# A cross-attention block on one core: the set-up copies, the constants' transfers and the last norms are rearranged

## The chip, the cores and the metric

The kernel runs on one core of one Trainium2 chip. The metric is the time of one execution on the device in microseconds (us). Engines are named as in the profile: PE is TensorE (matmuls; PEld its weight loads), DVE is VectorE, ACT is ScalarE, POOL is GpSimd, SP is SyncE, which here only issues transfers. ACT issues some transfers too; rows called SPq and ACTq are those issues. Each engine works through its own list of instructions strictly in the order in which the program gives them.

## The reference

One layer: 128 sequences of 128 tokens, model width 256, 16 heads of 16, feed-forward width 1024, everything float32.

```python
q = (x @ Wq + bq) ; k = (ctx @ Wk + bk) ; v = (ctx @ Wv + bv)      # 16 heads of 16
scores = einsum('bhqd,bhkd->bhqk', q, k) / sqrt(16)
scores = where(j < i, scores, -1e30)       # strictly below the diagonal
attn = softmax(scores); attn[:, :, 0, :] = 0
x1  = layer_norm(x + (attn @ v) @ Wo + bo, ln1_g, ln1_b)
out = layer_norm(x1 + relu(x1 @ W1 + b1) @ W2 + b2, ln2_g, ln2_b)
# layer_norm(t) = (t - mean) * (var + 1e-5) ** -0.5 * g + b
```

## The kernel before, in words

**Tiling.** Two sequences make a pair, and 64 pairs (p = 0 to 63) are worked through one after the other, software-pipelined by hand: while pair p has its scores and softmax, pair p-1 has its context, output projection and first norm, pair p-2 the first feed-forward matmul (`hidden`, result `hT`, through PSUM tile `ph`) and pair p-3 the second (`second`, PSUM tile `py`) with the last norm. The order on PE, DVE, ACT and POOL is the order of the calls in the program text; nothing is rescheduled.

**Softmax of a pair.** `scores(p, hi)` gives the upper (hi = 1) or lower half of the query rows in PSUM tile `pss`; DVE adds the mask tile `neg` while moving them to SBUF tile `sm` (L351), takes the negated maximum `nmx` (L362), POOL adds it (L363), ACT takes the exponential (L370), DVE sums (L382) and inverts (L383), and POOL multiplies (L384). The `sm` tiles have one buffer each. The weights are then turned: for most pairs by DVE and transfers (`turn`), for the first two and for part of the last on PE (`turn_on_pe`: four transposes into PSUM tile `ptp` at L426, then an ACT copy to `pT` at L428). `weigh` (PSUM `pc`), `context` (ACT, `cxT`) and `attention_out` (PSUM `po`) follow.

**Set-up.** Inputs come by transfers in the order of the text: on SP's queue the first tokens `x`, `wq`, `c_first` (the first pair's context), three `column` vectors (`bq_c`, `bk_c`, `b1_c`), weights `wk`, `wv`, `w1`, the blocks `xb`, `cb` of pair 1 (four transfers each), `wo`, rows, and the blocks of pairs 2 and 3; on ACT's queue three `chunks` (`bv_c`, `g1_c`, `be1_c`) and a copy of half of the mask, `neg` to `neg` (L169). Every transfer bears one of eight semaphores in rotation over both queues, and each issue waits until the transfer eight places earlier has landed. So the mask's copy waits for `be1_c`, and `wk` for `bv_c`; whatever is behind such a wait on its queue waits too. For pair 0, PE transposes `x` into `ptx` (L234), ACT copies it to `xT` (L671), PE projects queries into `pq` (L268), and then the same is done with `c_first` (`ptc`, `cT`) for the keys, `pk`. ACT moves `pq` to `qT` with bias `bqs_c` (L279) and `pk` to `kT` with `bkh` and `half` (L290). From pair 1 on, DVE makes `xT` and `cT` from the blocks (`tokens`, L253). `fold_norm1` (PSUM `ps_b`, L561) multiplies `w1` with `be1_c`; `fold_values` (`ps_bv`, L577; `bov_r`, L580) needs `bvw`, made from `bv_c`.

**Small PSUM tiles** (`bank`) share four buffers in rotation: `ptx`, `pq`, `pv`, `pc`, `po`, `ph`, `py`, `ptp` all come from them, and a matmul into a buffer waits until its previous content has been read.

**End.** In the last pair's turn of the loop (`end`) the lists are: `store` of an earlier pair's rows on ACT's queue, stats, `scale_and_shift` on POOL, then one half of `hidden(61)`, the transposes of pair 63's upper scores, the other half of `hidden(61)`, then `norm2` on ACT. After the loop pairs 61, 62 and 63 are finished one after the other; pair 62's last norm goes through `scale_and_shift` (POOL), `norm2` (ACT, L539), `finish` (POOL, L545 and L546); pair 63's goes sequence by sequence through the code at L886 to L904 on DVE and POOL, with a `pow` on POOL at L898.

Of the kernel before, what the change touches and what calls it, by code (L numbers as in the profile page):

```python
# [8 lines left out]
F32 = mybir.dt.float32  # L9
AF = mybir.ActivationFunctionType  # L10
ALU = mybir.AluOpType
AX = mybir.AxisListType

P = 128
NEG_INF = -1e30
# [4 lines left out]
def tile_cross_attention_block(  # L20
# [22 lines left out]
    nc = tc.nc  # L43
# [5 lines left out]
    KC = D // P  # L49
# [5 lines left out]
    HP = P // 2  # L55
    QSCALE = 1.0 / DK ** 0.5
# [6 lines left out]
    const = ctx.enter_context(tc.tile_pool(name="const", bufs=1))  # L63
# [11 lines left out]
    states = {}  # L75


    blocks_of, tokens_of = {}, {}
# [18 lines left out]
    def load_tokens(g, us=slice(0, 4)):  # L97
        if g not in tokens_of:
            tokens_of[g] = loads.tile([P, 4, D], F32, tag="x", name=f"x_{g}")
        nc.sync.dma_start(  # L100
            tokens_of[g][:, us], x[4 * g + us.start : 4 * g + us.stop].rearrange("b p d -> p b d")
        )


    def weight(w, name):
        n = w.shape[0] // P
        t = const.tile([P, n, w.shape[1]], F32, tag=name, name=name)
        nc.sync.dma_start(t, w.rearrange("(k p) n -> p k n", p=P))
        return t

    def column(v, name):
        t = const.tile([P, v.shape[1]], F32, tag=name, name=name)
        nc.sync.dma_start(t, v)
        return t

    def chunks(v, name):
# [4 lines left out]
    def row(v, name):  # L121
# [2 lines left out]
        return t  # L124

    load_tokens(0, slice(0, 2))
    c_first = const.tile([P, 2, D], F32, tag="c_first", name="c_first")
    wq = weight(Wq, "wq")
    nc.sync.dma_start(c_first, c[0:2].rearrange("b p d -> p b d"))
    bq_c = column(bq, "bq_c")  # L130
    bk_c = column(bk, "bk_c")
    wk = weight(Wk, "wk")
    wv = weight(Wv, "wv")
    ident = const.tile([P, P], F32, tag="ident", name="ident")
    make_identity(nc, ident)

    b1_c = column(b1, "b1_c")
    w1 = weight(W1, "w1")
# [14 lines left out]
    be2_r = row(ln2_b, "be2_r")  # L153
    be1b_r = const.tile([P, D], F32, tag="be1b_r", name="be1b_r")

    power = const.tile([P, 2, 1], F32, tag="power", name="power")
    nc.gpsimd.memset(power, -0.5)

    neg = const.tile([P, 2, HP], F32, tag="neg", name="neg")
    nc.gpsimd.memset(neg, 0.0)
    nc.gpsimd.affine_select(
        out=neg[:HP, 1, :], in_=neg[:HP, 1, :], compare_op=ALU.is_gt, fill=NEG_INF, base=0,
        pattern=[[-1, HP]], channel_multiplier=1,
    )
    nc.scalar.dma_start(neg[HP:, 1, :], neg[:HP, 1, :])  # L169

    live = const.tile([P, 1], F32, tag="live", name="live")
    nc.gpsimd.memset(live, 1.0)
# [16 lines left out]
            base=DK * e + DK - 1, pattern=[[32, NS]], channel_multiplier=-1,  # L189
        )  # L190
    nc.vector.tensor_reduce(half, half4, AX.X, ALU.add)

    bkh = const.tile([P, KC, 2], F32, tag="bkh", name="bkh")
    for m in range(KC):
        nc.vector.tensor_scalar(bkh[:, m, :], half, bk_c[:, m : m + 1], None, ALU.mult)

    bvw = const.tile([P, KC, P], F32, tag="bvw", name="bvw")
    nc.vector.tensor_copy(bvw, bv_c[:, :, None].to_broadcast([P, KC, P]))

    bqs_c = const.tile([P, KC], F32, tag="bqs_c", name="bqs_c")  # L200
    nc.vector.tensor_scalar(bqs_c, bq_c, QSCALE, None, ALU.mult)

# [15 lines left out]
    def bank(name):  # L221
        return ps_1.tile([P, 512], F32, tag="ps1", name=name)
# [302 lines left out]
    def scale_and_shift(p):  # L525

        st = states[p]
        deviation(p, 2)
        nb = st["nb"] = small.tile([P, 2, 1], F32, tag="nb", name=f"nb_{p}")
        for s in range(2):  # L530
            nc.gpsimd.tensor_scalar(
                nb[:, s], st["mv", 2][:, s, 0:1], st["sd", 2][:, s], -1.0, ALU.mult, ALU.mult
            )

    def norm2(p):
        st = states[p]
        t2, sd, nb = st["t2"], st["sd", 2], st["nb"]
        for s in range(2):
            nc.scalar.activation(  # L539
                t2[:, s], t2[:, s], AF.Identity, bias=nb[:, s], scale=sd[:, s]  # L540
            )

    def finish(p):
        t2 = states[p]["t2"]
        nc.gpsimd.tensor_tensor(t2, t2, g2_r[:, None, :].to_broadcast([P, 2, D]), ALU.mult)  # L545
        nc.gpsimd.tensor_tensor(t2, t2, be2_r[:, None, :].to_broadcast([P, 2, D]), ALU.add)  # L546

    def store(p):
        nc.scalar.dma_start(
            out[2 * p : 2 * p + 2].rearrange("b p d -> p b d"), states.pop(p)["t2"]  # L550
        )
# [109 lines left out]

    states[0] = {}
    for which, first, project_them in (
        ("x", tokens_of[0][:, 0:2], queries), ("c", c_first, keys)
    ):
        st = states[0]
        st[which + "T"] = proj.tile([P, KC, TP], F32, tag=which + "T", name=f"{which}T_0")
        pt = transposed(first, f"pt{which}_0")  # L670
        nc.scalar.copy(st[which + "T"].rearrange("p k i -> p (k i)"), pt)  # L671
        project_them(0)
    def feed(units):
        for what, p, part in units:
            if what == "hidden":
                hidden(p, range(part * FC // 2, (part + 1) * FC // 2))
            elif p in alone:
                second_alone(p, part)
            else:
                second(p, part)  # L680
# [98 lines left out]
    for p in range(2, NP):  # L779
        soon, end = p + 1 < NP, p == NP - 1  # L780
        first, then, finally_ = plan.get(
            p, ([("second", p - 3, 0)], [("second", p - 3, 1)], both("hidden", p - 2))
        )
        scores(p, 1)
        mask(p, 1, 0)
        maximum(p, 1, ONE)
        feed(first)
        mask(p, 1, 1)
        maximum(p, 1, TWO)
        scores(p, 0)  # L790
        mask(p, 0, 0)
        mask(p, 0, 1)
        exponential(p, 1, ONE)
        maximum(p, 0, ALL)
        exponential(p, 1, TWO)
        feed(then)
        sums(p, 1, ONE)
        sums(p, 1, TWO)
        summed = late + sum_up(first + then)
        exponential(p, 0, ALL)  # L800
        sums(p, 0, ALL)
        for q in waiting:
            finish(q)
        weigh(p - 1)
        context(p - 1)
        if soon:
            queries(p + 1)
        attention_out(p - 1)
        if not end:
            turn(p)  # L810
        attention_sum(p - 1)
        if soon:
            keys(p + 1)
        if p + 2 < NP:
            for which in "xc":
                tokens(p + 2, which)
        norm1(p - 1)
        if p > 4:
            turn_x1(p - 1)
        if soon:  # L820
            values(p + 1)
            values_out(p + 1)
        for q in waiting:
            store(q)
        if p == 2:
            turn_x1_on_pe(p - 1)
        residual1(p - 1)
        for q in summed:
            stats(q, states[q]["t2"], 2)
        if soon:  # L830
            add_bo(p + 1)
        if p % 2 == 0 and p + 4 < NP:
            load([p + 4, p + 5], "x")
            load_tokens(p // 2 + 2)
        if p % 2 == 1 and p + 3 < NP:
            load([p + 3, p + 4], "c")
        for q in summed:
            scale_and_shift(q)
        feed(finally_[:1])
        if end:  # L840
            turn_on_pe(p, 1, range(4))
        feed(finally_[1:])
        if p in (3, 4):
            turn_x1_on_pe(p - 1)
        late = sum_up(finally_)
        for q in summed:
            norm2(q)
        waiting = summed

    p = NP - 1  # L850
# [23 lines left out]
    second(p - 1, 1)  # L874
    second_sum(p - 1)
    stats(p - 1, states[p - 1]["t2"], 2)
    scale_and_shift(p - 1)
    norm2(p - 1)
    finish(p - 1)
    store(p - 1)  # L880

    st = states[NP - 1]
# [1 line left out]
    for s in range(2):  # L884
        py = bank(f"py_last_{s}")
        for f in range(FC):  # L886
            nc.tensor.matmul(
                py[:, :D], st["hT"][:, f, s * P : (s + 1) * P], w2[:, f, :],
                start=(f == 0), stop=(f == FC - 1),
            )  # L890
        nc.vector.tensor_tensor(t2[:, s], py[:, :D], st["x1b"][:, s], ALU.add)
        bs = small.tile([P, 6], F32, tag="bs", name=f"bs_last_{s}", bufs=4)
        mv = small.tile([P, 2], F32, tag="mvl", name=f"mv_last_{s}")
        nc.vector.bn_stats(bs, t2[:, s])
        nc.vector.bn_aggr(mv, bs)
        sd = small.tile([P, 1], F32, tag="sdl", name=f"sd_last_{s}")
        nc.gpsimd.tensor_scalar(sd, mv[:, 1:2], LN_EPS, None, ALU.add)
        nc.gpsimd.tensor_tensor(sd, sd, power[:, 0], ALU.pow)  # L898
        nc.vector.tensor_scalar(
            t2[:, s], t2[:, s], mv[:, 0:1], sd, ALU.subtract, ALU.mult  # L900
        )
        nc.vector.tensor_tensor(t2[:, s], t2[:, s], g2_r, ALU.mult)
        nc.vector.tensor_tensor(t2[:, s], t2[:, s], be2_r, ALU.add)
        nc.sync.dma_start(out[2 * NP - 2 + s], t2[:, s])  # L904


# [33 lines left out]
```

## Time and profile before

| | us |
|---|---|
| median of three runs | 1627.96 (1627.9, 1627.96, 1630.51) |
| profiled execution | 1631.7 |
| its span in the profile | 1630.0 |
| PE busy in the span | 1602.5 |
| DVE, POOL, ACT busy | 1312.8, 1276.6, 767.6 |
| first scores matmul of pair 0 begins | 19.04 |
| last matmul ends, about | 1621.1 |

A row of the timeline reads: start, duration, engine, line, operation, output<-input, shapes, number of instructions merged, and in brackets how long the engine sat idle before it and what ended the idling. A row of the chain of waits reads: start, duration, what the work that ended last was doing or waiting for then. "issue" is time in which the profile shows no cause.

### The profile page before, as it was taken

To read this page: it belongs to the slowest core of one execution; us is meant where nothing else is said; L and a number is where in the kernel's file an instruction comes from. 1 tells how busy PE (TensorE), PEld (TensorE's weight loads), DVE (VectorE), ACT (ScalarE), POOL (GpSimd) and SP (SyncE) were. 2 spreads that over 40 slices of the span, in tenths; PEclk is the share of its full clock that TensorE was granted. 3 is DMA by queue.
4 is the path that set the end of the run, shared out by engine and by line. 5 is a ranking of instruction groups with operands and counts; after the bars stand their busy time and mean duration, and the time that the engine had idled before them with its cause. 6 is when DMAs were issued, how large, how long until landed. Compare 5 with 4: busy or idle time off the path is not lost.

```text
span 1630.0 us, 41237 instructions
## 1 busy us (share of the span) xinstructions
PE 1602.5 (98%) x16520; PEld 1337.1 (82%) x16520; DVE 1312.8 (81%) x1984; ACT 767.6 (47%) x1503; POOL 1276.6 (78%) x1108
## 2 busy tenths in 40 slices
PE   7999999999999999999999999999999999999997
PEld 5778888888888888888888888888888888888876
DVE  4879888888888888888888888888888888888842
ACT  3554444444444544444544444444445445444442
POOL 4778887887887887887887887878878878878873
PEclk9999999999999999999999999999999999999999
DMA  7455655566565565665556655565565566556330
GB/s 146 92 114 119 138 134 133 134 134 141 132 140 129 131 141 138 132 134 135 129 138 137 133 133 134 130 147 131 134 136 135 127 142 138 133 132 137 93 89 20
DMA packets 480078, 208.80 MB, mean 128 GB/s; under 512 B 352145, under 2 KB 448401, under 8 KB 479889
## 3 DMA queue, kind: packets, MB, share of 16 engines
q1 hardware_dynamic: 395296, 181.25, 50.0%
q10 hardware_dynamic: 84592, 24.93, 6.4%
q8 instruction: 131, 2.15, 0.6%
q14 instruction: 59, 0.48, 0.1%
HBM read 69.48 MB, written 32.24 MB: 62 GB/s over the span
## 4 chain that ended last, share of the span: by engine, by line
PE 94%; DVE 2%; SPq 1%; POOL 1%; issue 1%; ACT 1%; DMA 1%; ACTq 0%; POOLq 0%; DVEq 0%
PE py L629 26%; PE ph L613 26%; PE pq L268 8%; PE pss L334 7%; PE pk L268 7%; PE po L472 7%; PE pv L300 7%; PE pc L453 3%; PE pc L443 2%; SPq L410 1%; PE py L641 1%; DVE sm L351 1%; DVE nmx L362 0%; PE ptp L426 0%; DMA be_c<-in_L_xattn_ln_b_dram 0%
## 5 line engine op out<-in xcount | busy, mean ns | idle before, releaser
L363 POOL TENSOR_TENSOR sm<-sm,nmx 128x1024 f32<-128x1024 f32 x192 | 364.5, 1899 | 196.5 <-DVE nmx L362 194.8
L613 PE MATMUL ph<-x1T,w 128*128 128x256 f32 x2048 | 454.4, 379 | 2.1 <-ACT x1T L603 2.1
L629 PE MATMUL py<-w,hT 128*128 128x256 f32 x1952 | 453.5, 385 | 0.0
L613 PEld LDWEIGHTS ph<-x1T,w 128*128 128x128 f32 x2048 | 388.4, 190 | 56.8 <-ACT x1T L603 3.2
L629 PEld LDWEIGHTS py<-w,hT 128*128 128x128 f32 x1952 | 361.0, 190 | 76.8 <-ACT hT L619 21.9
L351 DVE TENSOR_TENSOR sm<-pss,neg 128x1024 f32<-128x1024 f32 (+1 forms) x256 | 237.8, 950 | 200.8 <-PE pss L334 198.3
L370 ACT ACTIVATE sm<-sm 128x1024 f32<-128x1024 f32 x192 | 202.9, 1057 | 338.1 <-POOL sm L363 329.3
L384 POOL TENSOR_TENSOR sm<-sm,rs 128x1024 f32<-128x1024 f32 x192 | 359.4, 1900 | 2.8 <-DVE rs L383 2.8
L619 ACT ACTIVATE hT<-ph,b1e_c 128x256 f32<-128x256 f32 x512 | 214.5, 471 | 186.3 <-PE ph L613 151.0
L400 DVE STREAM_TRANSPOSE tb<-sm 128x1024 f32<-128x1024 f32 x183 | 220.4, 1230 | 33.2 <-POOL sm L384 23.7
L362 DVE TENSOR_REDUCE nmx<-sm 128x8 f32<-128x1024 f32 (+1 forms) x192 | 234.2, 1220 | 6.6
L382 DVE TENSOR_REDUCE su<-sm 128x8 f32<-128x1024 f32 (+1 forms) x192 | 229.5, 1195 | 1.1 <-ACT sm L370 0.8
L290 ACT ACTIVATE kT<-pk,bkh,half 128x256 f32<-128x256 f32 x256 | 123.8, 564 | 163.5 <-PE pk L268 163.5
L268 PE MATMUL pq<-xT,wq 128*128 128x256 f32 x512 | 131.1, 400 | 3.3 <-ACT xT L671 3.3
L334 PE MATMUL pss<-kT,qT 32*64 32x256 f32 (+1 forms) x4096 | 126.8, 335 | 1.8 <-ACT kT L290 1.3
L472 PE MATMUL po<-wo,cxT 128*128 128x256 f32 x512 | 121.3, 379 | 2.8 <-ACT cxT L465 1.4
L268 PE MATMUL pk<-cT,wk 128*128 128x256 f32 x512 | 123.3, 384 | 0.7 <-ACT cT L671 0.7
L518 POOL TENSOR_TENSOR x1b<-x,g_r 128x512 f32<-128x512 f32 x64 | 81.5, 1274 | 53.7 <-DVE x L510 53.7
L300 PE MATMUL pv<-wv,cT 128*128 128x256 f32 x512 | 121.1, 379 | 0.0
L334 PEld LDWEIGHTS pss<-kT,qT 32*64 32x64 f32 x4096 | 76.2, 131 | 49.3 <-issue 40.5
L268 PEld LDWEIGHTS pk<-cT,wk 128*128 128x128 f32 x512 | 98.8, 193 | 14.9 <-ACT cT L671 1.1
L268 PEld LDWEIGHTS pq<-xT,wq 128*128 128x128 f32 x512 | 94.2, 194 | 20.4 <-ACT xT L671 3.7
(82 smaller groups left out, 1688.9 us busy)
## 6 DMA issues: line engine op xcount, KB each, us to landing
pT<-tb SPq DMA_DIRECT2D x976, 96.0 KB, 2.2
out_dram<-t ACTq DMA_DIRECT2D x63, 256.0 KB, 4.1
xb<-in_x_dram SPq DMA_DIRECT2D x124, 128.0 KB, 4.5
cb<-in_ctx_dram SPq DMA_DIRECT2D x124, 128.0 KB, 4.1
x<-in_x_dram SPq DMA_DIRECT2D x31, 512.0 KB, 5.3
x1t<-tbx SPq DMA_DIRECT2D x236, 64.0 KB, 1.8
x1T<-x1t SPq DMA_DIRECT2D x59, 256.0 KB, 3.5
vd<-vz ACTq DMA_DIRECT2D x64, 128.0 KB, 3.8
```

Of the source, the lines that this page charges most:

```text
L268: nc.tensor.matmul(ps[:, m * TP : (m + 1) * TP], w[:, k, m * P : (m + 1) * P], src[:, k, :], start=(k == 0), stop=(k == KC - 1),)
L300: nc.tensor.matmul(pv[:, s * D : (s + 1) * D], st["cT"][:, k, s * P : (s + 1) * P], wv[:, k, :], start=(k == 0), stop=(k == KC - 1),)
L334: nc.tensor.matmul(sps[r // 2][s * HP : (s + 1) * HP, r % 2, m * 2 * n : (m + 1) * 2 * n].rearrange("p (e j) -> p e j", e=2), st["qT"][str ...
L351: nc.vector.tensor_tensor(st["sm", hi][:, part, :].rearrange("p (r n) j -> p r n j", r=2), st["sps", hi][t][:, :, : 4 * n].rearrange("p r ...
L362: nc.vector.tensor_reduce(nmx[:, part], sm[:, part, :], AX.X, ALU.max, negate=True)
L363: nc.gpsimd.tensor_tensor(sm[:, part, :], sm[:, part, :], nmx[:, part, None].to_broadcast([P, part.stop - part.start, n]), ALU.add,)
L382: nc.vector.tensor_reduce(su, sm[:, part, :], AX.X, ALU.add)
L384: nc.gpsimd.tensor_tensor(sm[:, part, :], sm[:, part, :], rs[:, :, None].to_broadcast([P, part.stop - part.start, n]), ALU.mult,)
L400: nc.vector.transpose(tb[:, :, at : at + 256].rearrange("p j (n a) -> p n j a", a=32), sm[:, t * 1024 : (t + 1) * 1024].rearrange("p (n j ...
L472: nc.tensor.matmul(po[:, s * D : (s + 1) * D], cxT[:, k, s, :], wo[:, k, :], start=(k == 0), stop=(k == KC - 1),)
L613: nc.tensor.matmul(ph[:, i * TP : (i + 1) * TP].rearrange("p (s i a) -> p s i a", s=2, a=32), w1[:, k, (f + i) * P : (f + i + 1) * P], st[ ...
L629: nc.tensor.matmul(st["py"][:, s * D : (s + 1) * D], st["hT"][:, f, s * P : (s + 1) * P], w2[:, f, :], start=(f == 0), stop=(f == FC - 1),)
```

## The change

For the first pair the PSUM copies of `xT` and `cT` go from ACT to DVE, both transposes come before both projections, and twelve transposes of the identity (`warm`) go ahead of them on PE. The three `column` transfers go from SP's queue to ACT's; an exponential of two elements (`table`) is put on ACT between them, so that its table is loaded there; the second half of the mask is made by a second POOL instruction instead of a transfer. The three small DVE operations (`bkh`, `bvw`, `bqs_c`) go behind the copies. In the last pair's turn of the loop both halves of `hidden(61)` go ahead of the transposes of pair 63's upper scores. The last norms of pairs 62 and 63 are done on DVE by `norm_alone`, two instructions for each sequence, with `deviation` on POOL ahead of them.

```diff
     def column(v, name):
-        nc.sync.dma_start(t, v)
+        nc.scalar.dma_start(t, v)
...
     load_tokens(0, slice(0, 2))
+    wq = weight(Wq, "wq")
     c_first = const.tile([P, 2, D], F32, tag="c_first", name="c_first")
-    wq = weight(Wq, "wq")
     nc.sync.dma_start(c_first, c[0:2].rearrange("b p d -> p b d"))
     bq_c = column(bq, "bq_c")
     bk_c = column(bk, "bk_c")
     wk = weight(Wk, "wk")
     wv = weight(Wv, "wv")
+    power = const.tile([P, 2, 1], F32, tag="power", name="power")
+    nc.gpsimd.memset(power, -0.5)
     ident = const.tile([P, P], F32, tag="ident", name="ident")
     make_identity(nc, ident)
+    table = const.tile([P, 2, 1], F32, tag="table", name="table")
+    nc.scalar.activation(table, power, AF.Exp)
     b1_c = column(b1, "b1_c")
...
-    nc.gpsimd.affine_select(
-        out=neg[:HP, 1, :], in_=neg[:HP, 1, :], compare_op=ALU.is_gt, fill=NEG_INF, base=0,
-        pattern=[[-1, HP]], channel_multiplier=1,
-    )
-    nc.scalar.dma_start(neg[HP:, 1, :], neg[:HP, 1, :])
+    for part in (slice(0, HP), slice(HP, P)):
+        nc.gpsimd.affine_select(
+            out=neg[part, 1, :], in_=neg[part, 1, :], compare_op=ALU.is_gt, fill=NEG_INF,
+            base=0, pattern=[[-1, HP]], channel_multiplier=1,
+        )
...
+    def norm_alone(t2, mean, sd):
+        nc.vector.scalar_tensor_tensor(t2, t2, mean, g2_r, ALU.subtract, ALU.mult)
+        nc.vector.scalar_tensor_tensor(t2, t2, sd, be2_r, ALU.mult, ALU.add)
...
+    warm = bank("warm")
+    for i in range(12):
+        nc.tensor.transpose(warm[:, i % 4 * P : (i % 4 + 1) * P], ident, ident)
     states[0] = {}
-    for which, first, project_them in (
-        ("x", tokens_of[0][:, 0:2], queries), ("c", c_first, keys)
-    ):
+    for which, first in (("x", tokens_of[0][:, 0:2]), ("c", c_first)):
         st = states[0]
         st[which + "T"] = proj.tile([P, KC, TP], F32, tag=which + "T", name=f"{which}T_0")
         pt = transposed(first, f"pt{which}_0")
-        nc.scalar.copy(st[which + "T"].rearrange("p k i -> p (k i)"), pt)
-        project_them(0)
+        nc.vector.tensor_copy(st[which + "T"].rearrange("p k i -> p (k i)"), pt)
+    for m in range(KC):
+        nc.vector.tensor_scalar(bkh[:, m, :], half, bk_c[:, m : m + 1], None, ALU.mult)
...
+    nc.vector.tensor_copy(bvw, bv_c[:, :, None].to_broadcast([P, KC, P]))
...
+    nc.vector.tensor_scalar(bqs_c, bq_c, QSCALE, None, ALU.mult)
+    queries(0)
+    keys(0)
...
-        feed(finally_[:1])
+        feed(finally_)
         if end:
             turn_on_pe(p, 1, range(4))
-        feed(finally_[1:])
...
     stats(p - 1, states[p - 1]["t2"], 2)
-    scale_and_shift(p - 1)
-    norm2(p - 1)
-    finish(p - 1)
+    deviation(p - 1, 2)
+    for s in range(2):
+        norm_alone(states[p - 1]["t2"][:, s], states[p - 1]["mv", 2][:, s, 0:1], states[p - 1]["sd", 2][:, s])
     store(p - 1)
...
         nc.gpsimd.tensor_tensor(sd, sd, power[:, 0], ALU.pow)
-        nc.vector.tensor_scalar(
-            t2[:, s], t2[:, s], mv[:, 0:1], sd, ALU.subtract, ALU.mult
-        )
-        nc.vector.tensor_tensor(t2[:, s], t2[:, s], g2_r, ALU.mult)
-        nc.vector.tensor_tensor(t2[:, s], t2[:, s], be2_r, ALU.add)
+        norm_alone(t2[:, s], mv[:, 0:1], sd)
         nc.sync.dma_start(out[2 * NP - 2 + s], t2[:, s])
```

More of the change, by code (lines that the diff above doesn't have):

```diff
@@ L154, in tile_cross_attention_block @@
     be1b_r = const.tile([P, D], F32, tag="be1b_r", name="be1b_r")
-    power = const.tile([P, 2, 1], F32, tag="power", name="power")
-    nc.gpsimd.memset(power, -0.5)
     neg = const.tile([P, 2, HP], F32, tag="neg", name="neg")
     nc.gpsimd.memset(neg, 0.0)
-    nc.gpsimd.affine_select(
-        out=neg[:HP, 1, :], in_=neg[:HP, 1, :], compare_op=ALU.is_gt, fill=NEG_INF, base=0,
-        pattern=[[-1, HP]], channel_multiplier=1,
-    )
-    nc.scalar.dma_start(neg[HP:, 1, :], neg[:HP, 1, :])
+    for part in (slice(0, HP), slice(HP, P)):
[3 more added lines that the diff above has]
+        )
     live = const.tile([P, 1], F32, tag="live", name="live")
@@ L191, in tile_cross_attention_block @@
     nc.vector.tensor_reduce(half, half4, AX.X, ALU.add)
[L193 to L201, printed above, removed]
     vzs, vds = [], []
@@ L670, in tile_cross_attention_block @@
         pt = transposed(first, f"pt{which}_0")
-        nc.scalar.copy(st[which + "T"].rearrange("p k i -> p (k i)"), pt)
-        project_them(0)
+        nc.vector.tensor_copy(st[which + "T"].rearrange("p k i -> p (k i)"), pt)
+    bkh = const.tile([P, KC, 2], F32, tag="bkh", name="bkh")
+    for m in range(KC):
+        nc.vector.tensor_scalar(bkh[:, m, :], half, bk_c[:, m : m + 1], None, ALU.mult)
+    bvw = const.tile([P, KC, P], F32, tag="bvw", name="bvw")
+    nc.vector.tensor_copy(bvw, bv_c[:, :, None].to_broadcast([P, KC, P]))
+    bqs_c = const.tile([P, KC], F32, tag="bqs_c", name="bqs_c")
+    nc.vector.tensor_scalar(bqs_c, bq_c, QSCALE, None, ALU.mult)
+    queries(0)
+    keys(0)
     def feed(units):
```

## The prediction

> **What bounds the kernel now.** First the page: busy time by engine, then the span in 40 slices.
>
> ```profile
> PE 1602.5 (98%) x16520; PEld 1337.1 (82%) x16520; DVE 1312.8 (81%) x1984; ACT 767.6 (47%) x1503; POOL 1276.6 (78%) x1108
> ...
> PE   7999999999999999999999999999999999999997
> ```
>
> PE is idle for 1630.0 − 1602.5 = 27.5 us in all, and its slices are full but for the first and the last. The change touches nothing in the 60 turns of the loop between. So it can only win at the two ends, and what PE wins at the start is kept as far as PE does not have to wait again before its steady state. Second, the chain of waits in the first 60 us:
>
> ```profile
> 1.85 4.41 DMA be_c<-in_L_xattn_ln_b_dram
> ...
> 8.21 0.59 ACT xT L671
> ...
> 8.84 3.79 PE pq L268 x8
> ...
> 14.15 3.80 PE pk L268 x8
> ...
> 20.65 1.92 PE pv L300 x8
> ```
>
> The first row is the wait of ACT's queue: the mask's copy (L169) can't be issued until `be1_c` has landed at 6.26, and the table load (1.28 us) and the copy of `xT` stand behind it. `ptx` was ready at 5.56, its copy ends at 8.80. Also, eight matmuls of `pq` or `pk` take 3.8 us and eight of `pv`, the same size, 1.92: the array ran at half rate until after `pk`. The windows print 1.00 for these first slices, but the clock's first record is a grant at 18.46; they print 0.50 from 25.28 to 32.11 (behind `fold_norm1`'s one-column matmuls), then 1.00.
>
> Third, the timeline at the end, where one pair has less PE work beside its softmax:
>
> ```profile
> 1574.58 0.38 ACTq L549 DMA_DIRECT2D out_dram<-t  x1
> ...
> 1575.01 1.57 ACT L619 ACTIVATE hT<-ph,b1e_c 128x256 f32<-128x256 f32 x4 [7.05 <-POOL ve L492]
> ```
>
> ACT stood for 7.05 us ahead of `hT` because the `store` before it on its queue waited for POOL's L546, done at 1574.55. PE's third `ptp` needs the buffer that this `hT` frees: after two of them, done at 1574.34, PE idles until 1575.95.
>
> **Start, part by part.** (a) DVE copies `ptx`: nearest row the PSUM read L498, 0.65 to 0.70 for 128x512. DVE has been free since `half` at 3.3. (b) The `warm` transposes: four of `ptx` take 1.09, so twelve take 3.27, from about 1.5 (`ident`, behind one more 0.1 memset) to 4.8; `ptx` runs 4.8 to 5.9 instead of 4.47 to 5.56, 0.3 later. (c) `ptc` follows when `c_first` lands (the landing records give 6.10), until 7.2; `xT` is copied meanwhile. `pq` starts at 7.25 instead of 8.84: −1.6. `cT` is copied beside `pq`, so `pk` follows at 11.05 instead of 14.15: −3.1. That is the floor, all at half rate.
>
> (d) The clock. [...]
>
> (e) What hides the rest. ACT's queue: two columns (0.5 each), the table load 1.28, an exponential of two elements (no such row: between 0.05 and 0.42, that of a 256-element `hT`), `b1_c`, `bv_c` issued near 3.9. Landing takes 3.8 to 4.4 like the other small ones, so `bv_c` at about 8.2, then `bvw` 0.29 and `bqs_c` 0.16 by 8.7. `qT` needs it when `pq` ends, 9.2 or later: hidden; later than that it costs one for one, up to the 3.8 of `pk`. `g1_c` waits for `x` (4.35), `be1_c` for `wq` (5.21): ACT is free at 5.75. POOL's extra mask half, 0.23, is hidden by 15 us of idle POOL. The queue of SP loses three issues (1.37) and the wait of 1.3 at `wk`, but then waits for `bk_c` at `w1`, which goes at 5.4 instead of 5.99. The transfers share 16 engines that are 0.7 to 1.0 busy there, so all blocks come about 0.6 earlier, no more.
>
> (f) That is the next bound:
>
> ```profile
> 24.66 5.97 SPq L93 DMA_DIRECT2D cb<-in_ctx_dram  x4
> ...
> 35.51 0.67 DVE L253 STREAM_TRANSPOSE cT<-cb 128x512 f32<-128x512 f32 x1
> ...
> 39.19 1.22 DVE L351 TENSOR_TENSOR sm<-pss,neg 128x1024 f32<-128x1024 f32 x1 [2.53 <-POOL xb L260]
> ```
>
> `cb` of pair 2 lands at 32.91; 0.6 earlier, 32.3. Then `cT` 0.67 and, behind it, `bov_r` (L580, 0.48) let the mask of pair 1 start at 33.5 at the earliest, instead of 39.19. So the start can bring 5.7 at most, and −4.4 fits under it: the 2.53 of idle DVE there takes the stall.
>
> **End, part by part.** (g) With all of `hidden(61)` first, PE goes on at 1573.4 without the wait: its two early buffers were those of `pc` and `po`, read by 1567.95 and 1570.73. It ends at about 1576.8. The four `ptp` then wait for `hT`, 0.39 each from 1575.01: last at 1578.2, so they end near 1578.9. The two of the lower half wait for `pT` copies (0.52 each from 1578.2) and end at 1579.9, and `second(61)` starts there instead of 1581.70: **−1.8**. Bounds: 0 if POOL's chain comes due again at `weigh`, −1.9 all of the idle time. ACT's `norm2` and lower `pT` copies end near 1582.9, `weigh` is at 1583.4: just covered. No transfer is moved.
>
> (h) The last norms.
>
> ```profile
> 1622.48 0.41 DVE L899 TENSOR_SCALAR t_last<-t_last,mv_last,sd_last 128x256 f32<-128x256 f32 x1 [3.53 <-POOL sd_last L898]
> 1622.93 0.42 DVE L902 TENSOR_TENSOR t_last<-t_last,g_r 128x256 f32<-128x256 f32 x1
> 1623.39 0.43 DVE L903 TENSOR_TENSOR t_last<-t_last,be_r 128x256 f32<-128x256 f32 x1
> 1623.73 0.42 DVE L891 TENSOR_TENSOR t_last<-py_last,x1b 128x256 f32<-128x256 f32 x1
> ```
>
> DVE waits 3.53 for `pow`, which on POOL stands behind `nb` and L545, L546 of pair 62 (0.50, 1.27, 1.26). These go, and 1.09 of ACT; DVE gets four instructions. A `scalar_tensor_tensor` from SBUF has no row; its neighbours are 0.41 and 0.48 (L580, from PSUM); I take 0.44. On the old clock: `sd` of pair 62 at 1617.29, four on DVE to 1619.1, then `t_last` of the first sequence 1619.5, statistics 1620.2, POOL 1621.2, two on DVE 1622.1. The second sequence (matmul done at 1621.1) starts its sum there instead of at 1623.73 and needs 3.0 instead of 3.45 to the end: 1625.1 instead of 1627.18, **−2.1**. At 0.41 it is −2.3, at 0.48 −1.8.
>
> **Sum.** −4.4 − 1.8 − 2.1 = −8.3, from the profiled 1631.7: 1623.4. [...] From 1630.51 the sum gives 1622.2, from 1627.9 1619.6. I say **1621.0**.
>
> **Rivals.** *Transposes count, loads bind* (0.22): the grant comes early, DVE waits for `cb`, the start gives 5.7, the sum −9.6: 1619.7. [...] *The start is given back* (0.20): the blocks land no earlier, or the half-rate stretch after `fold_norm1` falls on more of pair 1, and the start brings about 1, the ends 3.9: about 1623.5. For: transfers are saturated early; against: DVE's 2.53 of slack. *The last transposes come due* (0.10): `weigh` waits for what was put behind, (g) gives 0: 1622.8. *ACT's queue blocks* (0.04, slower): `be1_c` now stands ahead of `qT` and waits for the transfer eight places earlier. Before, `qT` started at 12.66; the gain of 3.9 at the end is used up when ACT comes free only at 16.5, and 0.2% slower needs 20. For: `neg`, issued at 6.34, took until 12.01 to land; against: `wq` landed at 5.21, eleven before that.
>
> **Numbers.** The forecast gets 0.44. A difference of 0.2% (3.3 us) is what a measurement here can tell. All cases but the last lie 4 to 8 under the median; a third of the given-back case, which sits nearest to the edge of 1624.7, I count as no change: faster 0.89, same 0.07, slower 0.04. The range is 1616.5 (loads less binding, best executions) to 1625.5 (half of the start lost, high execution).
>
> **What would show it.** `xT` copied by about 6.6 and `pq` starting near 7.25; `pk` at half rate at least in part, else the rule is wrong here; first `pss` near 14.7; the mask of pair 1 near 34.8 with DVE stalled at `cT` but not much; no idle PE around 1574, and `second(61)` 1.8 earlier against `hidden(61)`; the last output 4 us (not 6.1) behind the last matmul. I am wrong if `pss` begins after 17, or if PE shows new idle time between 20 and 60.

## The result, and the profile after

| | before | after |
|---|---|---|
| median, 10 runs each, us | 1629.02 (1627.64 to 1633.72) | 1624.05 (1621.81 to 1625.19) |
| profiled execution, us | 1631.7 | 1624.0 |
| its span, us | 1630.0 | 1622.2 |

The ratio is 0.9964, 95% interval [0.9954, 0.9973]: faster by 0.36%, 5.0 us in the medians, where 7 were forecast. The two profiled executions lie 7.7 apart, so a good part of what they differ by is no property of the two kernels. Lines of the changed kernel are numbered 9 lower in the helpers ahead of `norm_alone` (L351 is L342, L363 is L354) and 4 lower in those behind it (L580 is L576, L613 is L609).

The page of the changed kernel: PE as busy as before, in a span 7.8 shorter.

```profile
PE 1602.6 (99%) x16532; PEld 1338.3 (83%) x16532; DVE 1315.3 (81%) x1988; ACT 765.6 (47%) x1500; POOL 1274.9 (79%) x1105
...
PE 94%; SPq 3%; DVE 1%; DMA 1%; issue 1%; POOL 0%; ACT 0%; POOLq 0%; ACTq 0%; DVEq 0%
```

SP's queue, 1% of the chain before, is now 3%: the chain through the start has become one of transfers. The chain of waits of the changed kernel in its first 60 us says so:

```profile
27.75 4.51 DMA cb<-in_ctx_dram
...
33.10 0.44 DVE bov_r L576
33.54 1.14 DVE sm L342
...
38.07 0.93 issue
39.00 0.69 PE pss L325 x5
39.69 3.71 PE po L463 x8
43.40 2.16 PE pq L259 x8
...
50.01 3.72 PE ph L609 x16
```

The mask of pair 1 (the `sm` row) starts behind `cb` of pair 2 and is 5.7 earlier than before (33.46 in the timeline, against 39.19). But the first `ph` is only 3.6 earlier than in the chain of before:

```profile
53.58 3.72 PE ph L613 x16
```

Between the two, 2.1 are lost again. The eight matmuls of `po` take 3.71; eight of the same size, `pk` and `pv`, take 1.73 at full rate. The timeline of PE shows the other side, the very start:

```profile
1.45 2.82 PE L663 MATMUL warm<-ident 128*128 128x128 f32 x12 [1.45 <-POOL ident masks.py:199]
4.06 1.06 PE L225 MATMUL ptx<-ident,x 128*128 128x128 f32 x4
...
6.61 1.90 PE L259 MATMUL pq<-xT,wq 128*128 128x256 f32 x8
8.35 1.89 PE L259 MATMUL pk<-cT,wk 128*128 128x256 f32 x8
```

`pq` and `pk` run at full rate from their first matmul (1.90 and 1.89, against 3.78 each in the timeline of before): the clock's first record, one of full rate, begins at 6.61, and PE had run nothing but transposes until then. The windows of the same execution (length, busy time by engine, then granted clock, DMA share and GB/s) show the clock falling a second time, just where PE waits:

```profile
36.00:37.00 1.00, 0.00 (x0) 0.00 (x0) 1.00 (x1) 1.00 (x2) 0.91 (x1) 1.00 1.09 382
37.00:38.00 1.00, 0.89 (x23) 0.56 (x23) 0.97 (x2) 0.11 (x1) 0.99 (x1) 0.66 0.92 311
38.00:39.00 1.00, 0.07 (x4) 0.00 (x1) 0.31 (x1) 0.97 (x1) 0.61 (x1) 0.50 0.76 229
39.00:42.00 3.00, 3.00 (x11) 2.22 (x12) 2.39 (x3) 1.14 (x2) 1.28 (x1) 0.50 1.15 166
```

PE (first figure behind the length) does nothing from 36 to 37. In the 3.41 us ahead of the drop it is busy for 1.13; the record of half rate begins at 37.33 and lasts 6.83, to 44.16. PE's idle time between 20 and 60 is 4.2, against 2.8 before.

At the end, PE goes through `hidden(61)` without a stop, while before it stood 1.61 between the two pairs of transposes. First the timeline of before, then that of the changed kernel:

```profile
1569.84 3.62 PE L613 MATMUL ph<-x1T,w 128*128 128x256 f32 x16
...
1575.95 1.34 PE L426 MATMUL ptp<-ident,sm 128*128 128x128 f32 x8 [1.61 <-POOL sd L493]
...
1581.54 3.62 PE L629 MATMUL py<-w,hT 128*128 128x256 f32 x16
```

```profile
1566.66 7.07 PE L609 MATMUL ph<-x1T,w 128*128 128x256 f32 x32
...
1573.57 2.97 PE L417 MATMUL ptp<-ident,sm 128*128 128x128 f32 x24
...
1576.37 3.70 PE L625 MATMUL py<-w,hT 128*128 128x256 f32 x16
```

`second(61)` (`py`) starts 9.7 after the first `ph` of `hidden(61)` instead of 11.7. The timeline of the last norm in the changed kernel:

```profile
1617.61 0.48 DVE L541 SCALAR_TENSOR_TENSOR t_last<-t_last,mv_last,g_r 128x256 f32<-128x256 f32 x1
1617.67 0.51 POOL L907 TENSOR_SCALAR sd_last<-mv_last 128x1 f32<-128x1 f32 x1 [1.62 <-DVE mv_last L905]
1618.26 0.58 POOL L908 TENSOR_TENSOR sd_last<-sd_last,power 128x1 f32<-128x1 f32 x1
1618.88 0.48 DVE L542 SCALAR_TENSOR_TENSOR t_last<-t_last,sd_last,be_r 128x256 f32<-128x256 f32 x1 [0.78 <-POOL sd_last L908]
```

The first DVE pass runs beside POOL's `pow`. The last matmul ends at 1616.02 and DVE at 1619.36, 3.3 later instead of 6.1.

### The profile page after: what moved, and what is told of

It is laid out like the page before. It is cut to its first block, busy times and chain, and to the rows that moved or that the text cites. A ratio compares the mean times of both kernels' runs of the same rounds, so it can differ in the third digit from the quotient of the medians.

```text
span 1622.2 us, 41250 instructions
## 1 busy us (share of the span) xinstructions
PE 1602.6 (99%) x16532; PEld 1338.3 (83%) x16532; DVE 1315.3 (81%) x1988; ACT 765.6 (47%) x1500; POOL 1274.9 (79%) x1105
## 3 DMA queue, kind: packets, MB, share of 16 engines
q8 instruction: 132, 2.16, 0.6%
## 4 chain that ended last, share of the span: by engine, by line
PE 94%; SPq 3%; DVE 1%; DMA 1%; issue 1%; POOL 0%; ACT 0%; POOLq 0%; ACTq 0%; DVEq 0%
PE py L625 27%; PE ph L609 26%; PE pq L259 7%; PE po L463 7%; PE pss L325 7%; PE pk L259 7%; PE pv L291 6%; PE pc L444 3%; PE pc L434 2%; SPq L401 1%; SPq L93 1%; PE py L637 1%; DVE sm L342 1%; DVE nmx L353 0%; PE ptp L417 0%
## 5 line engine op out<-in xcount | busy, mean ns | idle before, releaser
L354 POOL TENSOR_TENSOR sm<-sm,nmx 128x1024 f32<-128x1024 f32 x192 | 364.5, 1899 | 189.2 <-DVE nmx L353 185.8
L609 PE MATMUL ph<-x1T,w 128*128 128x256 f32 x2048 | 454.1, 379 | 2.1 <-ACT x1T L599 2.1
L609 PEld LDWEIGHTS ph<-x1T,w 128*128 128x128 f32 x2048 | 388.5, 190 | 56.8 <-ACT x1T L599 3.2
L342 DVE TENSOR_TENSOR sm<-pss,neg 128x1024 f32<-128x1024 f32 (+1 forms) x256 | 237.7, 949 | 190.4 <-PE pss L325 190.4
L463 PEld LDWEIGHTS po<-wo,cxT 128*128 128x128 f32 x512 | 98.2, 192 | 15.4 <-ACT cxT L456 1.6
```

What stands on the lines that cost most here:

```text
L342: nc.vector.tensor_tensor(st["sm", hi][:, part, :].rearrange("p (r n) j -> p r n j", r=2), st["sps", hi][t][:, :, : 4 * n].rearrange("p r ...
L354: nc.gpsimd.tensor_tensor(sm[:, part, :], sm[:, part, :], nmx[:, part, None].to_broadcast([P, part.stop - part.start, n]), ALU.add,)
L463: nc.tensor.matmul(po[:, s * D : (s + 1) * D], cxT[:, k, s, :], wo[:, k, :], start=(k == 0), stop=(k == KC - 1),)
L609: nc.tensor.matmul(ph[:, i * TP : (i + 1) * TP].rearrange("p (s i a) -> p s i a", s=2, a=32), w1[:, k, (f + i) * P : (f + i + 1) * P], st[ ...
```

## The experiments

My theory after reading these profiles: the end is paid in full; the start is capped by `cb` of pair 2, and arriving there earlier only makes PE idle, and half rate follows (0.50 from 37.33 to 44.16). Rivals: the start's gain is a matter of where the clock's windows happen to fall (the records of the clock inside the two profiles last 3.41, 6.83 or 13.65 us, and the long ones, 1594.02 and 1576.96, are multiples of 3.41 too; such a stretch is called a window here); the transposes play no part in the clock.

**The end alone, the start alone.** `tail_only` is the kernel before with the diff's hunks of `feed` and `norm_alone`; `head_only` is the changed kernel with those undone:

```diff
-        feed(finally_[:1])
+        feed(finally_)
         if end:
             turn_on_pe(p, 1, range(4))
-        feed(finally_[1:])
...
-    scale_and_shift(p - 1)
-    norm2(p - 1)
-    finish(p - 1)
+    deviation(p - 1, 2)
```

> The kernel before with the edits of the end alone: hidden(61) ahead of the last pair's transposes, and the last norms by two DVE passes. Theory one (both edits of the end are paid in full and do not depend on the start): second(61) 2.0 us earlier against the first ph of hidden(61), the last DVE instruction 3.3 us behind the last matmul instead of 6.1, so 4.6 us less than before. Theory two (the end only takes up what the start has won, its stalls return): 2 us less or nothing.

> The changed kernel with the end as before. Theory one (the profiled pair is typical): the scores of pair 63 come 3.2 us earlier, the time is 3.2 us below before. Theory two (the start's gain depends on where the clock's free windows fall, and the profiled pair was a lucky one): between 0 and 1.5 us below before in the median, what is left of 5.0 when the end takes 4.6.

Measured: the end alone 1624.87 beside 1629.8 before, ratio 0.9965 [0.9951, 0.9978]: −4.9, theory one. The start alone 1628.62, ratio 0.9989 [0.9981, 0.9998]: −1.2, the number of theory two, though it doesn't yet tell chance in the windows from the cap. So nearly all of the change's gain is the end's, and the start hardly pays. `tail_only`, whose start is the old one, also shows how much an old start can differ from execution to execution: there `pk` ran at full rate (1.99 for 3.78), so did `pq` of pair 1 behind `fold_norm1` (1.99 for 3.78), and the first `ph` came at 48.87, against 53.58 in the profile of before. Part of this went again: that `ph` took 5.41 for 3.72, and its span is 7.2 shorter (1622.8 for 1630.0), of which the end is 4.7. So about 2.5 stayed: the profiled execution of before had a late start, and the sum was made against it.

**Without the twelve transposes.**

```diff
-    warm = bank("warm")
-    for i in range(12):
-        nc.tensor.transpose(warm[:, i % 4 * P : (i % 4 + 1) * P], ident, ident)
```

> The changed kernel without the twelve transposes of the identity. If transposes count for the clock: pq and most of pk at half rate (near 470 ns a matmul), pk ends 2.5 to 4.5 us later than the 10.1 of the changed kernel, but the mask of pair 1 still begins near 33.5, because it waits for cb of pair 2; the time within 1.5 us of the changed kernel. [...]

> The kernel without the transposes again, on the chip and beside the runs of before that the other three share: 1619.3 to 1621, below the changed kernel's range of 1621.8 to 1625.2; PE at full rate from the middle of pq or pk on and no second drop of the clock between 33 and 45.

Measured: 1620.07 (1619.35 to 1620.27), ratio 0.9935 [0.9921, 0.9948], and again 1618.78 (1617.78 to 1619.58), ratio 0.9932 [0.9919, 0.9946]. That is 4 to 5 below the changed kernel, with no overlap of the runs (about 4.8 and 6.2 when each is taken against its own runs of before); I had expected a difference of at most 1.5. The chain of waits of the first of the two:

```profile
7.53 3.41 PE pq L259 x8
10.94 1.86 PE pk L259 x8
...
33.11 1.14 DVE sm L342
...
46.83 3.72 PE ph L609 x16
```

`pq` is at half rate (3.41), as expected, and `pk` ends 2.5 later than in the changed kernel (12.8 against 10.2). The mask of pair 1 starts all the same at 33.03, and `ph` 3.2 earlier than in the changed kernel. What differs lies between: there is no second drop (in the timeline `po` and `pq` of pair 2 take 1.99 and 1.89, in the changed kernel 3.78 and 2.37), and in the view of waits (who waited for what: us in total, times, the longest), for PE from 30 to 55, the changed kernel has these at the top,

```profile
PE pss L325 <- DVE sm L342: 2.3, 2, 1.9
PE pss L325 <- issue: 0.9, 1, 0.9
```

and the one without transposes this for the mask, and no wait for "issue" at all:

```profile
PE pss L325 <- DVE sm L342: 0.7, 1, 0.7
```

In these two profiles the rows nearly close the sum. PE is idle for 1.2 more between 20 and 60 (4.17 against 2.94), and `po` and `pq` at half rate cost 2.4; the spans differ by 3.7 (1622.2, 1618.5). The timed runs, for which the mean granted clock is on record, agree in kind. The four of `no_warm` list 0.998. Two of the changed kernel's ten list 0.998 too and took 1621.87 and 1622.34; the other eight list 0.995 to 0.997 and have a median of 1624.2. So about 2 of the 4 to 5 go with the lower clock, and 2 or a little more are there without it.

**The start without them, the end as before.** The two edits undone together.

> The start's edits without the twelve transposes, with the end as before. If the transposes themselves spoil the start: 4 to 5.5 us below before (no_warm's 9.7 less the end's 4.9), against 1.2 with them. If no_warm's gain came from some interplay with the end: near the 1.2 of the start with them.

Measured: 1623.7, ratio 0.9962 [0.9949, 0.9976]: −6.3 beside a before of 1630.0. With the transposes the same start brought 1.2. So it is the transposes, not an interplay with the end; nor is it a chance of the windows in one execution, for with the transposes all eleven runs list a mean granted clock of 0.994 to 0.997, without them all four 0.997 or 0.998; and the −6.3 and −4.9 add up to the −11.2 of `no_warm_again`, which was measured beside the same runs of before as the −6.3.

**Do transposes count for the clock?**

```diff
-    for i in range(12):
+    for i in range(48):
```

> The changed kernel with 48 transposes of the identity instead of twelve: PE does nothing but transposes until past 8. If transposes count for the clock: within them the time of one falls from about 235 ns to about 130, at the latest 6.9 us after they begin, and a record of full rate begins there. If they don't count: all 48 take about 235 ns and pq starts at half rate.

> The changed kernel with 48 transposes for twelve, now timed. If it is arriving early at the wait for cb that costs the time (idle PE, clock drop, code not yet loaded), this later start gives 1 to 3.5 us less than the changed kernel although its first scores come 4 us later. If every us of the start counts: 3 to 4 us more.

The timeline of `warm48`:

```profile
1.44 7.94 PE L663 MATMUL warm<-ident 128*128 128x128 f32 x48 [1.44 <-POOL ident masks.py:199]
9.22 0.60 PE L225 MATMUL ptx<-ident,x 128*128 128x128 f32 x4
...
10.61 1.99 PE L259 MATMUL pq<-xT,wq 128*128 128x256 f32 x8 [0.35 <-DVE xT L669]
```

At 235 ns each (2.82 for twelve), 48 would take 11.3; they took 7.94. By that length full rate came near 6.5, in their midst, about 5 after they began (an estimate from the rows: 0.22 from one to the next in the twelve, 0.11 in the `ptx` behind them; the 6.9 of the expectation was an estimate too, no run shows it as a bound). So transposes count here: of the eight profiles that have these transposes ahead, six have the first `pq` at full rate from its start (1.89 to 1.99; `queries2_early` has 2.29, `tokens2_late` 3.25). And though the first scores come 4.1 later than in the changed kernel (15.44 against 11.35), the time is not longer: 1620.85 in this execution, 1622.04 (1619.81 to 1623.87) in the four runs of `warm48_again`, ratio 0.9952 [0.9938, 0.9965]. These 4.1 us of an early start are worth nothing here.

**Transfers that come late.** Three transfers that nothing needs before the first norm of pair 0 go behind the blocks of pairs 2 and 3:

```diff
-    load_tokens(0, slice(2, 4))
-    g1_r = row(ln1_g, "g1_r")
-    be1_r = row(ln1_b, "be1_r")
...
     load([2, 3])
+    load_tokens(0, slice(2, 4))
+    g1_r = row(ln1_g, "g1_r")
+    be1_r = row(ln1_b, "be1_r")
     load_tokens(1)
```

> The changed kernel with three transfers (second half of the first tokens, g1_r, be1_r) put behind the blocks of pairs 2 and 3 on SP's queue. If cb of pair 2 sets the mask of pair 1: cb lands 1.5 to 3 us earlier, the mask begins near 32.1 (PE's transposes come due) and the time falls by 1 to 3 us. If the transfers are not what is late: no change within 0.5 us.

> No twelve transposes, and the three transfers behind the blocks of pairs 2 and 3: the two changes that helped, together. If both help by letting the mask of pair 1 come when PE is ready: cb no longer waited for, the mask at about 32.4, 0.5 to 1.5 us below the 1620.1 without transposes. If PE's code or DVE's chain is the bound by then: the same as without transposes, within 0.5.

Measured: with the transposes 1618.63 (1618.5 to 1621.58, the profiled one), ratio 0.9932 [0.9915, 0.9948]; `po` is at full rate (1.99 in the timeline, where the changed kernel has 3.78), and `cb` is no longer what the mask of pair 1 waits for (the `cT` row came at 32.46 in the changed kernel):

```profile
28.48 0.71 DVE L244 STREAM_TRANSPOSE cT<-cb 128x512 f32<-128x512 f32 x1
...
32.48 1.23 DVE L342 TENSOR_TENSOR sm<-pss,neg 128x1024 f32<-128x1024 f32 x1 [2.53 <-PE ptp L417]
```

Without the transposes 1619.88, ratio 0.9940 [0.9927, 0.9954], no better than without them alone; the mask is at 32.29, behind PE's transposes of the weights (`ptp`). Put together:

| median, us | rows ahead of the blocks | rows behind |
|---|---|---|
| twelve transposes | 1624.05 | 1618.63 |
| none | 1620.07, 1618.78 | 1619.88 |

The transposes cost 4 to 5 us where `cb` comes late and nothing where it doesn't. Either of the two edits gives the best kernels found, which beat both the kernel before and the changed one.

**Other ways to mend the stretch, which failed.** All three start from the changed kernel. `gap_filled` keeps PE busy:

```diff
     context(0)
+    gap = bank("gap")
+    for i in range(12):
+        nc.tensor.transpose(gap[:, i % 4 * P : (i % 4 + 1) * P], ident, ident)
     scores(1, 0)
```

`queries2_early` puts real work there:

```diff
     context(0)
+    queries(2)
     scores(1, 0)
...
     attention_sum(0)
-    queries(2)
```

`tokens2_late` takes the wait for `cb` out of DVE's way to the masks:

```diff
-    for which in "xc":
-        tokens(2, which)
...
     maximum(1, 0, ALL)
+    for which in "xc":
+        tokens(2, which)
     attention_out(0)
```

> The changed kernel with twelve more transposes of the identity (1.6 us at full rate) on PE between weigh(0) and scores(1, 0), where PE stands idle for the mask of pair 1. They do no useful work. If the clock's drop there costs the time: no record of half rate between 34 and 45, po and pq of pair 2 at 1.73 to 1.9 for eight, the time 2 to 4 us below the changed kernel, near 1620 to 1621.5. If the wait itself costs it: the time the same within 0.7 us, or up to 1.6 us longer.

> The changed kernel with queries(2) moved into the same idle stretch, between weigh(0) and scores(1, 0): real work instead of transposes. If PE's idle time and the clock are what is lost there: 1.7 us for the moved matmuls and the clock's 2 to 3 us, the time 3 to 5 us below the changed kernel. If only the idle time: 1 to 1.7 us below. If the stretch is set by DVE and POOL and not by PE: the same.

> The changed kernel with pair 2's two DVE transposes put behind the three masks and maxima of pair 1. If DVE waiting for cb of pair 2 sets the mask of pair 1: the mask begins near 32.1, when PE has turned the weights of pair 0, and PE idles less between 32 and 39; the time falls by 1 to 3 us. If something else sets it (PE's transposes, POOL): the mask stays near 33.5 and the time the same within 0.5 us.

Measured 1622.96, 1623.79 and 1623.22, ratios 0.9959 [0.9944, 0.9974], 0.9962 [0.9947, 0.9977] and 0.9954 [0.9942, 0.9967]: none clear of the changed kernel. In each, what was aimed at did happen. `gap_filled` has `po` and `pq` at full rate (1.99 and 1.89). `queries2_early` filled the gap and has `po` at full rate (1.99), but its first `ph` takes 5.41 for 3.72 instead. `tokens2_late` has the mask at 31.64. But in their place came waits for "issue", here `gap_filled`:

```profile
PE pss L325 <- issue: 3.0, 1, 3.0
PE ptn L225 <- DVE x L501: 0.9, 1, 0.9
```

The wait for "issue" is 2.5 in `tokens2_late` and 0.5 in `queries2_early`, where `ptn` waits 2.4 for DVE besides. So the second drop of the clock is not the sole loss: PE also waits there for something that the profile puts down to no engine.

## Why the prediction was right, and which step was wrong

Time, direction and range held, but with errors that partly offset each other: the sum of parts was −8.3, the medians moved by −5.0, the start brought a quarter of its share and the end more than its own. That the time still fell inside the range is partly luck, for its upper end stood for half of the start lost. And one of the prediction's own signs of being wrong came true: new idle time on PE between 20 and 60 (4.2, against 2.8).

- **(a) to (c), copies and order:** right. `x` and `c_first` landed about 0.4 earlier than in the profile of before and the twelve transposes took 2.82 for 3.27, so `pq` began at 6.61 (forecast 7.25).
- **(d), the clock:** the wrong choice, against *Transposes count*. The −4.4 stands for `pk` ending at 13.55 instead of 17.95, on a clock that transposes don't help; it was my estimate, and no run shows it. What the runs showed in its place: in the changed kernel full rate came at 6.61, when all that PE had run were transposes, and with the 48 it came within them (7.94 where 11.3 was due). `pk` ended at 10.2, 7.7 earlier than before, and the start alone measured −1.2. Without the transposes `pk` ended at 12.8.
- **(e), the hidden costs:** right. `bqs_c` was done at 8.05 (forecast 8.7), because ACT's table load (1.80 to 3.08) ran beside its next two transfer issues (1.86 and 2.31) and not ahead of them.
- **(f), the cap by `cb`:** right to the tenth, 33.46 for 33.5. But the mask itself was forecast at 34.8, short of the cap, and it met the cap, even in `no_warm` (33.03), where `pk` ended at 12.8.
- **What failed is the sentence on the cap,** that 4.4 "fits under it" because DVE's slack takes the stall. DVE's did; PE's did not. PE came to the scores of pair 1 early and waited 2.3 for masks and 0.9 for "issue". The clock dropped behind this idle stretch (1.13 busy of 3.41), and `po` took 1.98 longer and `pq` 0.43 (3.71 and 2.16 for 1.73). The forecast −4.4 for the start measured −1.2. Among the rivals, this is "the start is given back" (about 1), whose stated cause, the half-rate stretch behind `fold_norm1`, was not the one: it was a second such stretch, behind the wait, together with the waits themselves.
- **(g), `hidden(61)` first:** −1.8 forecast, −2.0 in the rows, a little beyond its own bound of −1.9; the idle row that went is 1.61.
- **(h), the norms:** −2.1 forecast, −2.7 in the rows. Mis-sized: I let both passes wait for `sd`, but the first needs only the mean and runs beside POOL's `pow`. Passes took 0.45 to 0.48 for the assumed 0.44. Together −4.7; the end alone measured −4.9.
- **The base.** I started from 1627.9 to 1630.5; ten runs gave a median of 1629.02. With −1.2 and −4.9 the sum is 1622.9, inside the runs of the changed kernel.

Still open: what each of the second drop, the wait for masks and the wait for "issue" would be worth by itself. The division above is read from single executions and from mean clocks, and the three attempts to remove one at a time brought another. Whether the twelve transposes matter also because they shift the place where the "issue" wait falls was not tried by itself.

## What to carry to other kernels

A gain at the start is worth only what the next transfer lets through, and here a PE that arrived early did not just wait: a stretch with little PE work (1.13 busy of 3.41) was followed by matmuls at half rate (`po` 3.71 for 1.73). So find the landing that is due next before warming or hastening anything ahead of it, and move that transfer first; here the order of three transfers on one queue was worth as much as taking the warm-up out. At the end of this kernel, where only a short chain of work stood behind the last matmuls, the gain was what the rows had said (−4.7 in the rows, −4.9 measured).

## What the runs showed of the hardware

- Full rate came after transposes alone: at 6.61 in the changed kernel, where PE had run nothing else, and within the 48 of `warm48` (7.94 where 11.3 was due). In six of the eight profiles with transposes ahead the first `pq` took 1.89 to 1.99; in `queries2_early` and `tokens2_late`, with the same twelve, it took 2.29 and 3.25, so full rate came only during it.
- Half rate came during or soon after `fold_norm1`'s 32 one-column matmuls (3.63 to 4.49 us): in 13 of 14 profiles the `pq` of pair 1 behind them took 3.11 to 3.78. In the profile of before the record of half rate begins at 25.27, among the 32, and lasts 6.83; in the changed kernel it begins at 20.26, 1.9 after them, and lasts 3.41. In the fourteenth (`tail_only`) that `pq` took 1.99; what set it apart was not shown.
- The waits for "issue" on PE ended 1.4 to 1.7 after a 16 KB packet of the DMA queue that the profile calls "instruction" had ended: at 44.93 and 46.38 before, 37.37 and 39.00 in the changed kernel, 39.34 and 40.84 in `gap_filled`. What these waits are for was not shown.
- The first full rate came at different times with the same twelve transposes, begun at 1.45: near 4.2 in `head_only` (`ptx`, begun at 4.06, took 0.66 for 1.06), at 6.61 in the changed kernel, near 9.8 in `tokens2_late` (`pq`, begun at 7.07, took 3.25 for 1.89). The first and the last are estimates from these lengths.
